# Layer 1 of a two-layer cross-attention kernel: keys, tokens and cluster tiles turned on VectorE and through DRAM instead of on TensorE

## The chip, the cores and the metric

One core of a Trainium2 chip. The metric is device microseconds (us) of one execution of the whole program, float32 throughout. The kernel before ran three times: 1796.07, 1797.0 and 1801.03 us, median 1797.0. Engines in the views: PE is TensorE's matrix multiplication, PEld its weight loads, DVE is VectorE, ACT ScalarE, POOL GpSimd, SP SyncE, which here does nothing but issue DMAs.

## The reference

`x` is 32 batches of 64 tokens of 512 elements, `ctx` the same shape. Two layers run one after the other, each with an attention to `ctx` and a feed-forward part. Layer 0 (one wide attention head, a sparse feed-forward part) is not touched by the change. Layer 1 is:

```
def xattn(h, ctx):                     # h = layernorm(x)
    q = (h @ Wq.T)  -> 32 heads of 128
    k = (ctx @ Wk.T), v = (ctx @ Wv.T) -> 8 groups of 128
    q = rmsnorm(q) * q_norm_w          # over the 128 of a head
    k = rmsnorm(k) * k_norm_w          # each group serves 4 heads
    p = softmax(q @ k.T / sqrt(128) + mask)
    return (p @ v) @ Wo.T
def ffn(h):                            # h = layernorm(x), 2048 rows
    dots = softmax(h @ centroids.T / 0.1)         # 64 clusters
    hits = dots > 0.01
    row_sel = any(hits over rows)[assignments]    # per output column
    query_sel = any(hits over clusters)           # per row
    return where(query_sel & row_sel, h @ weight.T + bias, 0)
x = x + xattn(layernorm(x), ctx)
x = x + ffn(layernorm(x))
```

## The kernel before

**Residency.** `x` stays in SBUF as 16 tiles `X[t]` of 128 rows (two batches) by 512. A matrix product contracts over the 128 partitions, so whatever enters a product must first stand "turned", with the contracted dimension on partitions. Before, this turning is a TensorE transpose: a matmul against the identity matrix from SBUF into PSUM, followed by a copy back to SBUF on ScalarE or VectorE. `transposed` (L181 its matmul) does four of them for a 128x512 tile.

**Units.** Layer 1 is cut into 32 units: T = 0 to 3 (512 tokens each, eight batches) by g = 0 to 7 (a key and value group with its four query heads). The four large projections are done by Winograd's scheme: seven products of 2x2 blocks in place of eight, with sums of inputs formed on GpSimd (`four_sums`, L127), each product two halves of four matmuls of 128x256 into a PSUM bank `b` (L901). One product takes TensorE 1.73 us, one projection 12.1 us.

- `project_kv` runs for every second unit and makes keys and values of two groups, in the layout tokens on partitions (`kv`).
- `project_q` runs for each unit and makes the turned queries `qT` from the turned, normalised tokens `xt` and their sums `tx`.
- `normed_keys`, `applied_norms` and `turned_keys` run once per pair of units: sums of squares of the keys, the reciprocal root (`ss`), a product `kn = kv * ss` (L1022), four transposes into PSUM `ptk` (L1033), and a scaling from PSUM by the column `wkc` (both norm weights and the 1/sqrt(128)) into `kT` (L1035), twice.
- `query_norms` gets the queries' sums of squares with small matmuls (L1048) and a VectorE transpose by 32x32 blocks (L1054).
- `softmax` has 32 small matmuls of 64x64 per half (L1070), `turn` turns the probabilities by 32x32 blocks on VectorE and DMAs between partitions (L1108 and L1116), `attend` multiplies by the values (L1130), `project_out` adds into `X` (L1161).

**Order.** The loop over units is a hand-written software pipeline: in iteration n stand the attention of unit n-1, the scores of unit n, `project_kv` (for an even g) and `project_q` of unit n+1, then `project_out` of unit n-1, in the middle of which the keys of the next pair were turned. `tc.issue_after` pins an instruction behind another on the same or another engine; what is not pinned is placed by a list scheduler. SP issues its DMAs in one order for the whole program, and a DMA that waits holds all behind it. Weights for T = 0 come from the inputs, with their sums made on GpSimd and stored to DRAM (`keep_sum`, L887); for T = 1 to 3 they are read (L880).

**Tokens.** `tokens(T)` normalises four tiles of `X` (`layernorm`: L104, L105, L114, L115 and L108 for `xn`), transposes them in the midst of `project_kv` (`amid`), copies them to `xt` on ScalarE (L924) and sums on GpSimd. For T = 0 this stands at the start of layer 1, with no other unit beside it.

**Clusters.** For tiles 0 to 11, `turn_and_keep` normalises the finished `X[t]`, transposes it (L181, `pt4`), copies it to `xT4` (L1182) and writes that to DRAM (`XTS`); `clusters` multiplies it with the centroids `CE` (L1198, `pl`) a unit later, two tiles at a time, in units 25 to 30. After the loop the twelve tiles are read back (L1316) for the dense product `pd` (L1350); tiles 12 to 15 are turned in the tail.

**Buffers.** The work tag `xn1` has two buffers of 128x512 and serves `xn` and, in the last unit, one half of `tb`. The PSUM tag `p1` has two banks, shared by `ptx`, `ptk1`, `pt4`, `pl` and half of the attention's results.

Of the kernel before, what the change touches and what calls it, by code (L numbers as in the profile page):

```python
# [16 lines left out]
P = 128  # L17
# [18 lines left out]
def tile_kernel(  # L36
# [801 lines left out]
    with ExitStack() as pc:  # L838
# [16 lines left out]
        ones32 = wk.tile([P, 32], F32, name="ones32", bufs=1)  # L855
        nc.vector.memset(ones32, 1.0)

        first_sums, context_sums, kv_products, softmaxes, projected = [], [], [], [], []
# [48 lines left out]
        def sbuf_keep(n, ps):  # L907
            e = wk.tile([P, 2, 256], F32, name=f"keep{n}", tag="keep", bufs=4)
            keeps.append(nc.scalar.copy(e, ps).ins)  # L909
            return e  # L910

        def tokens(T):


            xt = cpool.tile([P, C, 512], F32, name=f"xt_{T}", tag="xt")

            def normed(k):
                for a in (2 * k, 2 * k + 1):
                    xn = wk.tile([P, D], F32, name="xn1", tag="xn1")
                    layernorm(xn, 4 * T + a)  # L920
                    pt = ps_1.tile([P, C, P], F32, name="ptx", tag="p1")
                    with tc.issue_after(kv_products[2 if T == 0 else -1]):
                        transposed(pt, xn)
                    nc.scalar.copy(xt[:, :, a * P : (a + 1) * P], pt)  # L924

            def summed():
                q = [xt[:, 2 * i : 2 * i + 2, 256 * j : 256 * j + 256] for i in range(2) for j in range(2)]
                s = [cpool.tile([P, 2, 256], F32, name=f"tx_{T}_{k}", tag=f"tx_{k}") for k in range(4)]

                with tc.issue_after(context_sums[0]) if T == 0 else ExitStack():  # L930
                    first_sums.append(four_sums(nc.gpsimd, s, *q, True))
                return q + s

            return normed, summed

# [8 lines left out]

        def project_kv(cts, gp, T, amid=None):

# [4 lines left out]
            def mm(i, ps, first):  # L951
                if amid is not None and i in (7, 3):
                    amid((7, 3).index(i))
                last = products(ps, lambda h, c: cts[LEFT[i]][:, h, c, :], lambda h, c: w[i][:, c, :], first)
                kv_products.append(last.ins)
                projected.append(last.ins)
                if T == 0:
                    keep_sum(w, i, WKS, gp, True, last)
# [53 lines left out]

        def applied_norms(kvs, ss, behind, rooted):

            with tc.issue_after(rooted) if rooted is not None else ExitStack():
                nc.scalar.activation(ss, ss, AF.Sqrt, bias=eps5, scale=1.0 / HD)
            with tc.issue_after(behind[0]), tc.issue_after(behind[-1]):
                nc.vector.reciprocal(ss, ss)
            kns = []
            for k, kv in enumerate(kvs):  # L1020
                kn = wk.tile([P, 4, HD], F32, name="kn", tag="ksq", bufs=2)
                nc.vector.tensor_mul(kn, kv[:, :, 0:HD], ss[:, k, :, None].to_broadcast([P, 4, HD]))  # L1022
                kns.append(kn)
            return kns

        def turned_keys(kns, behind):

            kTs = []
            for kn in kns:
                pt = ps_1.tile([P, 4, P], F32, name="ptk1", tag="p1")  # L1030
                for a in range(4):
                    with tc.issue_after(behind):
                        nc.tensor.transpose(pt[:, a, :], kn[:, a, :], ident)  # L1033
                kT = wk.tile([P, 512], F32, name="kT1", tag="kT1")
                nc.vector.tensor_scalar(kT, pt.rearrange("p a t -> p (a t)"), wkc, None, ALU.mult)  # L1035
                kTs.append(kT)
            return kTs
# [22 lines left out]
        def softmax(h, qT, kT, ss, behind):  # L1060
# [3 lines left out]
            for a in range(2):  # L1064
                for j in range(J):
                    for b in range(2):
                        bb = 2 * (2 * h + a) + b
                        at = 2 * (2 * h + b) + a
                        with tc.issue_after(behind):
                            score = nc.tensor.matmul(  # L1070
                                sc[b * S : (b + 1) * S, 4 * a + j, :], qT[:, at, j, :],
                                kT[:, bb * S : (bb + 1) * S], start=True, stop=True,
                            )
# [99 lines left out]
        hit = wk.tile([P, NT], F32, name="hit", bufs=1)  # L1173
        XTS = [dram.tile([P, C, P], F32, name=f"xts_{t}", tag=f"xts_{t}") for t in range(12)]

        def turned(t, out, behind=None):
            xn = wk.tile([P, D], F32, name="xn1", tag="xn1")
            applied.append(layernorm(xn, t))
            pt = ps_1.tile([P, C, P], F32, name="pt4", tag="p1")
            with tc.issue_after(behind) if behind is not None else ExitStack():  # L1180
                transposed(pt, xn)
            nc.scalar.copy(out, pt)  # L1182

        def turn_and_keep(t):
            out = wk.tile([P, C, P], F32, name="xT4", tag="xT4", bufs=2)
            turned(t, out)
            nc.sync.dma_start(XTS[t], out)
            return out

        def clusters(t, tiles, behind=None):  # L1190

            pl = ps_1.tile([P, 2, NCL], F32, name="pl", tag="p1")
            for m in range(2):
                for c in range(C):
                    for k in range(2):
                        half = slice(k * P // 2, (k + 1) * P // 2)
                        with tc.issue_after(behind) if behind is not None else ExitStack():
                            nc.tensor.matmul(  # L1198
                                pl[half, m, :], tiles[m][:, c, half], CE[:, c, :], start=c == 0,
                                stop=c == C - 1, skip_group_check=True,  # L1200
# [32 lines left out]
        with tc.high_priority(offset=100):  # L1233
            normed, sums_of = tokens(0)
            normed(0)
            normed(1)
            xts = sums_of()
        kns = normed_keys(kvs)
        qT, qsq = project_q(xts, 0, 0)
        kTs = turned_keys(applied_norms(kvs, kns, puts[:1], None), projected[-3])  # L1240
        kT = kTs[0]
# [10 lines left out]
        for n, (T, g) in enumerate(units):  # L1252
# [14 lines left out]
            if more:  # L1267
# [3 lines left out]
                if g2 == 0:  # L1271
                    normed, sums_of = tokens(T2)
                    kvs = project_kv(cts, 0, T2, normed)
                    xts = sums_of()
# [19 lines left out]
            if more and g2 % 2 == 0:  # L1294
                with tc.high_priority(offset=60):
                    kTs = turned_keys(
                        applied_norms(kvs, kns, puts[-2:], keeps[-2]), outs[-5] if before is not None else projected[-1]
                    )
            kT = kTs[g2 % 2]
# [4 lines left out]
            t = 2 * (n - 24)  # L1304
            pair = (t, [turn_and_keep(t), turn_and_keep(t + 1)]) if 0 <= t < 12 else None
            if n == 23:
# [6 lines left out]
        nc.sync.dma_start(WD, wd)  # L1313
        xT = [fpool.tile([P, C, P], F32, name=f"xT4_{t}") for t in range(NT)]
        for t in range(12):
            nc.sync.dma_start(xT[t], XTS[t])  # L1316
        bdb = wk.tile([P, D], F32, name="bdb", tag="rt", bufs=1)
# [24 lines left out]
        def dense(t, parts=1):  # L1342


            for h in range(parts):
                cols = slice(D // parts * h, D // parts * (h + 1))
                pd = ps_j.tile([P, D // parts], F32, name="pd", tag="pj")
                for c in range(C):
                    with tc.issue_after(dense_at[-1]) if dense_at else ExitStack():
                        ins = nc.tensor.matmul(  # L1350
                            pd, xT[t][:, c, :], WD[:, c, cols], start=c == 0, stop=c == C - 1
                        )
# [150 lines left out]
```

## Time and profile before

The profile is of one execution, which took 1799.84 us; its span, from the first to the last instruction, is 1798.1 us, with 1.74 us around it.

| what | value |
|---|---|
| time of the profiled execution / its span | 1799.84 us / 1798.1 us |
| median of the runs | 1797.0 us |
| layer 0, up to the first layer 1 matmul | 556.16 us from the span's start |
| one period of layer 1 (two units) | 71.58 us |
| PE busy | 1773.8 us, 11364 instructions |
| VectorE / ScalarE / GpSimd busy | 968.0 / 623.0 / 715.4 us |
| DMA | 219.31 MB, mean 122 GB/s |
| granted TensorE clock, mean | 0.999 of full speed |

How to read it: busy time of an engine is the sum of its instructions' listed durations, overlaps counted once. A matmul's end is modelled, so that what PE really spends on a row of matmuls is the distance between starts. A line of a timeline has the start, the duration, the engine, the source line, the operation, the tiles written and read, the shapes, and the count of instructions merged; a bracket gives idle time before it and what ended that. In the table by stretches each engine has its busy time and, in brackets, its instructions; the last three numbers are the granted clock, the share of the DMA engines' time and GB/s. The chain of waits follows the last instruction back to what released it, step by step.

### The profile page before, as it was taken

The numbers are of one execution on the slowest core, as the hardware profiler recorded it, in microseconds if no ns is written. First come the engines' busy times: TensorE is split into PE (matmuls) and PEld (weight loads), VectorE is DVE, ScalarE is ACT, GpSimd is POOL, SyncE is SP. The second block draws the span as 40 slices with busy tenths as digits, with TensorE's granted clock in tenths as the row PEclk, the third lists the DMA queues.
The fourth block names the chain that finished last, engine by engine and source line by source line (L and its number), as shares of the span: only waits on it lengthen the run. The fifth ranks groups of instructions, "written<-read, shape, count | busy, mean of one in ns | idle before, by whom it ended". The sixth has DMA issues, their size and how long they took to land.

```text
span 1798.1 us, 29543 instructions
## 1 busy us (share of the span) xinstructions
PE 1773.8 (99%) x11364; PEld 1446.9 (80%) x11364; DVE 968.0 (54%) x1733; ACT 623.0 (35%) x1157; POOL 715.4 (40%) x622
## 2 busy tenths in 40 slices
PE   8999999999999999999999999999999999999999
PEld 4544988988998788888888888888888888888864
DVE  5887565555524454455455444555554555555557
ACT  4654322222112423334234333442343433433311
POOL 1552433443327766764324234332243332322320
PEclk9999999999999999999999999999999999999999
DMA  9632400000014344454444454444445444443513
GB/s 248 195 108 66 166 23 22 22 22 21 13 55 148 130 158 152 141 194 153 147 147 130 143 162 126 132 147 136 135 131 163 137 129 143 149 146 117 182 48 94
DMA packets 169500, 219.31 MB, mean 122 GB/s; under 512 B 19024, under 2 KB 108112, under 8 KB 168720
## 3 DMA queue, kind: packets, MB, share of 16 engines
q1 hardware_dynamic: 155712, 206.91, 37.1%
q10 hardware_dynamic: 13648, 10.50, 2.0%
q8 instruction: 91, 1.49, 0.4%
q14 instruction: 49, 0.40, 0.1%
HBM read 176.74 MB, written 32.21 MB: 116 GB/s over the span
## 4 chain that ended last, share of the span: by engine, by line
PE 88%; POOL 4%; DMA 3%; DVE 2%; ACT 1%; issue 1%; SPq 0%; POOLq 0%; ACTq 0%; DVEq 0%
PE b L901 49%; PE ph L727 10%; PE po L770 10%; PE pv L1130 3%; PE sc L1070 3%; PE pd L1350 3%; PE pq L397 3%; POOL so L127 2%; PE pk L374 2%; PE pr L1048 1%; PE pt L181 1%; PE pi L279 1%; POOL prob L1077 1%; DMA x<-in_x 1%; DMA wos<-wo 1%; PE ptk L1033 1%
## 5 line engine op out<-in xcount | busy, mean ns | idle before, releaser
L1161 DVE TENSOR_TENSOR x<-x,b 128x512 f32<-128x512 f32 x224 | 153.9, 687 | 228.7 <-PE b L901 228.7
L127 POOL TENSOR_TENSOR so<-oT 128x512 f32<-128x512 f32 x64 | 80.1, 1273 | 485.0 <-ACT oT L1137 485.0
L901 PE MATMUL b<-tx,wq 128*128 128x256 f32 x1024 | 237.8, 380 | 3.2 <-DVE qT L994 1.7
L901 PE MATMUL b<-wo,so 128*128 128x256 f32 x1024 | 231.7, 379 | 1.8 <-issue 1.8
L901 PEld LDWEIGHTS b<-tx,wq 128*128 128x128 f32 x1024 | 193.9, 190 | 31.9 <-POOL tx L127 2.5
L901 PEld LDWEIGHTS b<-wo,so 128*128 128x128 f32 x1024 | 194.5, 190 | 28.6 <-issue 2.2
L901 PE MATMUL b<-xt,wq 128*128 128x256 f32 x768 | 183.5, 381 | 0.9 <-DVE kv L965 0.9
L901 PE MATMUL b<-wo,oT 128*128 128x256 f32 x768 | 181.5, 379 | 0.0
L901 PEld LDWEIGHTS b<-xt,wq 128*128 128x128 f32 x768 | 144.4, 190 | 21.2 <-DVE kv L965 1.3
L901 PEld LDWEIGHTS b<-wo,oT 128*128 128x128 f32 x768 | 144.8, 190 | 19.9 <-issue 1.0
L909 ACT COPY keep<-b 128x512 f32<-128x512 f32 x144 | 83.8, 583 | 181.7 <-PE b L901 178.8
L1137 ACT COPY oT<-pv 128x512 f32<-128x512 f32 x64 | 37.4, 584 | 280.6 <-PE pv L1130 270.8
L994 DVE TENSOR_TENSOR qT<-b,keep 128x512 f32<-128x512 f32 x96 | 66.1, 689 | 116.9 <-PE b L901 114.5
L901 PE MATMUL b<-wkv,sc 128*128 128x256 f32 x512 | 117.0, 380 | 0.0
L1082 DVE TENSOR_REDUCE mx<-prob 128x8 f32<-128x512 f32 x64 | 43.9, 686 | 125.0 <-POOL prob L1077 125.0
L901 PEld LDWEIGHTS b<-wkv,sc 128*128 128x128 f32 x512 | 96.6, 190 | 13.8 <-issue 1.0
L272 POOL TENSOR_TENSOR e<-e,down 128x896 f32<-128x896 f32 (+1 forms) x40 | 68.0, 1706 | 93.9 <-DVE e L268 89.8
L997 ACT ACTIVATE qsq<-qT 128x512 f32<-128x512 f32 x128 | 80.3, 627 | 70.5 <-DVE qT L994 58.6
L770 PE MATMUL po<-w,gT 128*128 128x256 f32 x448 | 101.9, 382 | 0.0
L1094 POOL TENSOR_TENSOR prob<-prob,mx 128x512 f32<-128x512 f32 x64 | 66.5, 1060 | 86.0 <-DVE mx L1093 83.6
L770 PEld LDWEIGHTS po<-w,gT 128*128 128x128 f32 x448 | 84.0, 190 | 18.7 <-issue 7.8
L901 PE MATMUL b<-wkv,ct 128*128 128x256 f32 x384 | 93.0, 384 | 2.6 <-DVE mx L1093 2.0
(211 smaller groups left out, 3053.0 us busy)
## 6 DMA issues: line engine op xcount, KB each, us to landing
wq<-in_wq SPq DMA_DIRECT2D x104, 256.0 KB
wo<-in_wo SPq DMA_DIRECT2D x104, 256.0 KB
wq<-wqs SPq DMA_DIRECT2D x96, 256.0 KB
wo<-wos SPq DMA_DIRECT2D x96, 256.0 KB
wkv<-in_wkv SPq DMA_DIRECT2D x52, 256.0 KB
wkv<-wks SPq DMA_DIRECT2D x48, 256.0 KB
wqs<-wq SPq DMA_DIRECT2D x32, 256.0 KB
aT<-tb ACTq DMA_DIRECT2D x256, 32.0 KB
```

The costliest lines, as they stand in the source:

```text
L127: ins = eng.tensor_tensor(s[k], *pairs[k], op)
L272: nc.gpsimd.tensor_tensor(e3, e3, down[:, None, :].to_broadcast([P, k, BLK]), ALU.mult)
L397: nc.tensor.matmul(pq, xT[:, tt, c, :], WQ[:, c, :], start=c == 0, stop=c == C - 1)
L727: nc.tensor.matmul(ps[:, c, :], W1[LEFT[i]][:, d, (c0 + c) * P : (c0 + c + 1) * P], xq[RIGHT[i]][:, d, :], start=first and c == 0 and d == ...
L770: nc.tensor.matmul(ps, chunk(gq[LEFT[i]], c), W2[RIGHT[i]][:, c, :], start=first and c == 0, stop=c == HC - 1, skip_group_check=True,)
L901: last = nc.tensor.matmul(out[:, h, :], lhs(h, c), rhs(h, c), start=first and h == 0 and c == 0, stop=c == 1, skip_group_check=True,)
L909: keeps.append(nc.scalar.copy(e, ps).ins)
L994: ins = nc.vector.tensor_add(o, ps, kept.rearrange("p j (b t) -> p j b t", t=S))
L997: nc.scalar.activation(qsq[:, 4 * th : 4 * th + 4, 2 * hh : 2 * hh + 2, :], o, AF.Square)
L1070: score = nc.tensor.matmul(sc[b * S : (b + 1) * S, 4 * a + j, :], qT[:, at, j, :], kT[:, bb * S : (bb + 1) * S], start=True, stop=True,)
L1094: ins = nc.gpsimd.tensor_tensor(pr, pr, mx[:, 1, :, None].to_broadcast([P, 8, S]), ALU.mult)
L1161: added.append(nc.vector.tensor_add(xq[:, i, j], xq[:, i, j], ps).ins)
```

## The change

Everything that layer 1 turned on TensorE before tile 12 of the clusters is turned in another way: VectorE transposes a 128x512 tile by 32x32 blocks, with the blocks put in an order that makes rows of 128 elements (`to_dram`), SP writes the 256 KB to DRAM, and four DMAs read it back into 32 partitions each (`from_dram`), in pieces of 512 bytes. The two steps together are the whole transpose.

- Keys: `applied_norms` and `turned_keys` become one function. The norm weights are no longer a column after the transpose; they are a row `wkrow`, the same on all partitions, multiplied in with the norm by a `scalar_tensor_tensor` per head of 128. `wkrow` is made once, by four small matmuls `pw` of `ones32` with the diagonal matrix `wkd`, and four copies. `kT` now lies as `[p, q, a, x]`, in runs of 32.
- Tokens: `norm_tokens` normalises and writes `XND[T]`; for T = 1 to 3 it is called in units g = 4 and 5 of the T before. `tokens` reads it. `xt` lies as `[p, 16, c, 32]`; the sums use views of it, and `tx` has the layout as before.
- Clusters: tiles 0 to 11 go through `XTS`, which now is one tensor, and are read back for `clusters` at once and again after the loop. Their layout is `[p, row, c]`, so that the stationary operand of `pl` and `pd` takes every fourth element. `xT` becomes one tile, `xTs`, of all 16; tiles 12 to 15 still use TensorE, and their copies write the new layout.

In the changed kernel's order of TensorE, the four `pw` stand after the last matmul of layer 0 and before the first product of `project_kv`.

```diff
+        wkd = wk.tile([P, P], F32, name="wkd", tag="xn1")
+        nc.vector.tensor_scalar(wkd, ident, wkc, None, ALU.mult)
+        wkrow = wk.tile([P, HD], F32, name="wkrow", bufs=1)
+        for r in range(4):
+            pw = ps_1.tile([32, P], F32, name="pw", tag="p1")
+            nc.tensor.matmul(pw, ones32, wkd, start=True, stop=True)
+            nc.scalar.copy(wkrow[32 * r : 32 * r + 32, :], pw)
...
+        def to_dram(rows, src, order, name):
+            tb = wk.tile([P, D], F32, name=name, tag="xn1")
+            to = {"c h": "p (h c x) -> p c h x", "x c": "p (h x c) -> p c h x"}
+            nc.vector.transpose(
+                tb.rearrange(to[order], h=4, x=32), src.rearrange("p (c h x) -> p c h x", h=4, x=32)
+            )
+            return nc.sync.dma_start(rows, tb)
+        def from_dram(dst, rows):
+            for h in range(4):
+                nc.sync.dma_start(
+                    dst[32 * h : 32 * h + 32],
+                    rows[:, P * h : P * h + P].rearrange("(q l) x -> l q x", l=32),
+                )
+        def norm_tokens(T, a):
+            xn = wk.tile([P, D], F32, name="xn1", tag="xn1")
+            layernorm(xn, 4 * T + a)
+            to_dram(XND[T][a * P : (a + 1) * P, :], xn, "c h", "tbx")
...
         def tokens(T):
-                    with tc.issue_after(kv_products[2 if T == 0 else -1]):
-                        transposed(pt, xn)
-                    nc.scalar.copy(xt[:, :, a * P : (a + 1) * P], pt)
+            xt = cpool.tile([P, 16, C, 32], F32, name=f"xt_{T}", tag="xt")
+            from_dram(xt.rearrange("p q c x -> p q (c x)"), XND[T])
...
-                nc.vector.tensor_mul(kn, kv[:, :, 0:HD], ss[:, k, :, None].to_broadcast([P, 4, HD]))
...
-                        nc.tensor.transpose(pt[:, a, :], kn[:, a, :], ident)
-                kT = wk.tile([P, 512], F32, name="kT1", tag="kT1")
-                nc.vector.tensor_scalar(kT, pt.rearrange("p a t -> p (a t)"), wkc, None, ALU.mult)
+                for a in range(4):
+                    nc.vector.scalar_tensor_tensor(
+                        kn[:, a, :], kv[:, a, 0:HD], ss[:, k, a : a + 1], wkrow, ALU.mult, ALU.mult
+                    )
+                to_dram(KTD[k], kn.rearrange("p a d -> p (a d)"), "c h", "tbk")
+                kT = wk.tile([P, 4, 4, 32], F32, name="kT1", tag="kT1")
+                from_dram(kT.rearrange("p q a x -> p q (a x)"), KTD[k])
...
         def turn_and_keep(t):
-            out = wk.tile([P, C, P], F32, name="xT4", tag="xT4", bufs=2)
-            turned(t, out)
-            nc.sync.dma_start(XTS[t], out)
+            for m in range(2):
+                xn = wk.tile([P, D], F32, name="xn1", tag="xn1")
+                layernorm(xn, t + m)
+                to_dram(XTS[(t + m) * P : (t + m + 1) * P, :], xn, "x c", "tbc")
+            out = wk.tile([P, 2, P, C], F32, name="xT4", tag="xT4", bufs=1)
+            from_dram(out.rearrange("p m (q x) c -> p (m q) (x c)", x=32), XTS[t * P : (t + 2) * P, :])
...
-                                pl[half, m, :], tiles[m][:, c, half], CE[:, c, :], start=c == 0,
+                                pl[half, m, :], tiles[m][:, half, c], CE[:, c, :], start=c == 0,
...
+            if T < 3 and g in (4, 5):
+                for a in (2 * g - 8, 2 * g - 7):
+                    norm_tokens(T + 1, a)
...
-        xT = [fpool.tile([P, C, P], F32, name=f"xT4_{t}") for t in range(NT)]
-        for t in range(12):
-            nc.sync.dma_start(xT[t], XTS[t])
+        xTs = fpool.tile([P, NT, P, C], F32, name="xTs")
+        for t, n in ((0, 2), (2, 4), (6, 6)):
+            from_dram(
+                xTs[:, t : t + n].rearrange("p m (q x) c -> p (m q) (x c)", x=32), XTS[t * P : (t + n) * P, :]
+            )
...
-                            pd, xT[t][:, c, :], WD[:, c, cols], start=c == 0, stop=c == C - 1
+                            pd, xT[t][:, :, c], WD[:, c, cols], start=c == 0, stop=c == C - 1
```

## The prediction

> **What bounds the kernel now.** I read the page's first part, then the chain, then a table by stretches, then timelines where the edits land. The first two, from the page:
>
> ```profile
> PE 1773.8 (99%) x11364; PEld 1446.9 (80%) x11364; DVE 968.0 (54%) x1733; ACT 623.0 (35%) x1157; POOL 715.4 (40%) x622
> ...
> PE 88%; POOL 4%; DMA 3%; DVE 2%; ACT 1%; issue 1%; SPq 0%; POOLq 0%; ACTq 0%; DVEq 0%
> ```
>
> The table by stretches, here for one period of layer 1 (two units of work):
>
> ```profile
> core 0: us, PE busy (x) PEld busy (x) DVE busy (x) ACT busy (x) POOL busy (x), PEclk, DMA share, GB/s
> ...
> 1003.17:1074.75 71.58, 71.58 (x465) 61.00 (x464) 35.27 (x58) 25.85 (x41) 27.97 (x24) 1.00 0.51 151
> ```
>
> PE holds 88% of the chain, and in the period it is busy throughout at a granted clock of 1.00, while VectorE is busy for 35.27 of 71.58 us and the DMA engines for half. So in the steady part PE time taken away is time saved, and VectorE has 36 us free per period. Only the edges of layer 1 are not of this kind.
>
> **What is removed.** PE loses 240 transposes: 128 of keys, 64 of tokens, 48 for the cluster tiles 0 to 11. Their listed 273 ns is no price, since modelled ends overlap. The price is the step between starts, on PE's timeline (start, duration, count last):
>
> ```profile
> 1002.31 1.03 PE L901 MATMUL b<-wo,so 128*128 128x256 f32 x4
> 1003.17 1.04 PE L1033 MATMUL ptk<-ident,kn 128*128 128x128 f32 x8
> 1004.04 1.89 PE L901 MATMUL b<-wo,oT 128*128 128x256 f32 x8
> ```
>
> Eight transposes hold PE from 1003.17 to 1004.04: 0.87 us, or 109 ns each. Keys: 16 such groups, 13.9 us. Tokens: 64 x 0.109 = 7.0. Cluster tiles: 48 x 0.109 = 5.2. Together **-26.1 us**. With T=1's token copies ACT is also freed; on PE's timeline 0.90 us is lost at 844.13, waiting for ACT's `keep` in that stretch: **-1**.
>
> VectorE loses 32 `kT` scalings (L1035, 22.5 us) and 32 products `kn` (L1022, 22.9). It gains 60 block transposes, at the 704 ns of L1108's `tb`, 42 us, and 128 products of 128x128. No row shows that product; L744's 384-element form takes 609 ns and its 512-element form 746, so a line through them gives about 0.26 us, 33 us in all. Net +30 us on an engine busy for 968 of 1798.
>
> **Keys, in the steady part: hidden.** They now go VectorE, DRAM, SBUF. In the period shown the reciprocal of the keys' norms runs at 997.07. Eight products and two transposes (8 x 0.26 + 2 x 0.70), interleaved with x's additions, end at about 999.2 and 1001.3. A 256 KB write takes about 2 us from issue to the last packet (the `wo` load issued at 1003.37 ends at 1005.6), so the copies lie in DRAM at 1001 and 1003.2. Eight reads follow on SP, 0.33 to 0.38 us each to issue, and about 1 us for 512 packets: `kT` is there at about 1005 and 1006. The first score starts at 1013.97, 0.87 earlier once the transposes are gone. Slack: **7 us**. Behind these DMAs on SP stands the weight load issued at 1001.64, now about 1005.3; its product is a whole unit later. Cost 0.
>
> Tokens of T=1 to 3 are written one to two units ahead and read about 17 us before their use: 0. Cluster tiles of one pair keep only 2 to 3 us of slack, the others a unit: 0, with a bound of +3.
>
> **T=0: the part that shows.** Here no unit runs beside the chain. Before, PE's order is:
>
> ```profile
> 553.14 3.18 PE L770 MATMUL po<-w,gT 128*128 128x256 f32 x14
> 556.16 1.89 PE L901 MATMUL b<-wkv,ct 128*128 128x256 f32 x8
> ...
> 568.40 1.89 PE L901 MATMUL b<-wkv,ct 128*128 128x256 f32 x8
> 570.13 1.89 PE L901 MATMUL b<-xt,wq 128*128 128x256 f32 x8
> ```
>
> and what VectorE and GpSimd do in it:
>
> ```profile
> 555.29 2.49 POOL L127 TENSOR_TENSOR sc<-ct 128x512 f32<-128x512 f32 x2 [5.20 <-DMA ct<-in_cT]
> ...
> 556.36 0.42 DVE L778 TENSOR_TENSOR x<-x,po 128x256 f32<-128x256 f32 x1 [1.69 <-PE po L770]
> 556.70 1.10 DVE L853 TENSOR_TENSOR wkc<-colt 128x1 f32<-128x1 f32 x1
> ...
> 557.75 1.27 POOL L127 TENSOR_TENSOR sc<-sc,ct 128x512 f32<-128x512 f32 x1
> ```
>
> First, the four matmuls `pw` of the key weights' row stand in PE's order ahead of `project_kv`. They wait for `wkd`, which follows `wkc` on VectorE; the 128x1 product took 1.10 us, to the end of GpSimd's two sums at 557.78, and `wkd` likewise waits for the third, which ends at 559.0. Then four matmuls go with copies between them (two PSUM buffers, L461's 266 ns): keys' projection starts at 559.6 to 560.5 instead of 556.16, **3.4 to 4.3 us late**.
>
> Second, the token chain. Without 16 transposes `project_kv` would end at 568.4, and 4 us later at 572.4; then `project_q` needs `xt`. Each of four tiles takes a normalisation, a transpose and a write of about 2 us, and the transposes share two buffers with what they read, so each waits for the write before it: about 2.2 to 2.7 us a tile from 560.5. The last write is issued at about 568 to 570.5 and landed 2 us later. Then the reads: 2048 packets of 512 B. The nearest row is `ch<-choice` (64 KB issues at 171.26 to 178.7, 512-B packets): 1792 packets in 8.0 us, 224 per us, and 400 per us at its densest. So 5.1 to 9.1 us, and `xt` is there at 575.5 to 581; I take 577.5, from the early write and a rate near 350, since four large issues leave no gaps as the sixteen small ones do. Against 568.4 the whole boundary costs **+9.1** (7 to 13).
>
> Third, the clock. The table by stretches after an earlier place with gaps (third number from the right: granted clock):
>
> ```profile
> 178.90:182.40 3.50, 3.50 (x16) 1.89 (x15) 3.20 (x6) 0.00 (x0) 2.17 (x2) 0.51 0.86 262
> 182.40:190.00 7.60, 7.60 (x70) 7.60 (x70) 2.10 (x5) 2.32 (x5) 0.00 (x0) 1.00 1.05 396
> ```
>
> After gaps of about 1 us between 174 and 180 the granted clock was 0.51 for 3.5 us, a loss of 1.7. Two idle stretches of 4 to 5 us may each do this: 0 to 3.4, I take **+1.7**. The weight loads and GpSimd's sums of T=0 run in another order against `project_q`; **+1** (-2 to +4).
>
> **Stationary operands at a 16-byte stride.** Cluster tiles now lie as `[p, row, c]`, so 256 weight loads of `pl` and 136 of `pd` pick every fourth element. No row of before has this. Below: 0, as nothing in it shortens a load. Above: `pl` runs at a 29 ns step (32 in 1.0 us from 1479.76), and were its loads four times as long as that step, 256 x 87 = 22 us. `pd` has a 429 ns step over loads listed at 190, so up to twice nothing shows. Nearest in kind are L1130 and L1048, whose moving operand comes in runs of 32 at no cost (390 against L901's 380), but runs are not single elements. I take a tenth of the upper end, **+2.5**, range 0 to 22.
>
> [...]
>
> **Tail.** `xTs` is one tile; its twelve reads become 6144 packets of 512 B, 15 to 27 us by the rates above from about 1688, and the `wo` loads stand behind them on SP (before issued from 1697.75). They are wanted at 1711.54, where 1.82 us is already lost: **+1** (0 to 6).
>
> **Sum.** -26.1 - 1 + 9.1 + 1.7 + 1 + 2.5 + 1 = -11.8. The profiled execution took 1799.84 us (span 1798.1 and 1.74 around it): 1788.0. It lies 2.8 above the median of the runs, 1797.0, so in medians **1785**. All favourable ends together give -22, 1775; all unfavourable ones, with the cluster tiles' +3 but the stride at 0, give +2, 1799.
>
> **Rivals.**
> 1. The T=0 chain is hidden (GpSimd's sums or other loads bind there anyway, `pw` is early): -11.8 - 10 = -22, **1775**. For: VectorE has free time. Against: `pw` is first in PE's order.
> 2. The boundary and the tail take their upper ends (+13, +3.4, +4, +6) and `pl`'s step grows by half (+4): -26.1 - 1 + 30.4 = +3, or **1800**: no change. For: writes and reads in series with two buffers. Against: it wants all of them late.
> 3. Slower: the keys' round trip. Each write, read and wait on SP's one queue is longer than I take it, because SP waits at the first write for VectorE and at the reads for the write's landing, with weight loads around them. It decides when `kT` lands over 7 us later than my 1006, a round trip of 14 us from the last transpose's 1001.3 to 1013.1 in place of 5. Each us later than that is paid in each of the 15 pairs after the first: 2 us late is 1785 + 30 = **1815**. For: every hop is serial and unshown. Against: the wait for DMA engines is small at a share of 0.51.
> 4. PE's work is not really less (the order puts other work in the transposes' place): **1797**. The instruction list speaks against it; a few in a hundred.
>
> **Chances.** Forecast (1777 to 1792) 0.60, first rival 0.11, second 0.14, third 0.12, fourth 0.03. A measurement here tells about 0.3% (5.4 us) from no change. Faster by more: 0.74 (forecast, first rival, a little of the second); within: 0.14; slower: 0.12. For 8 in 10 the range takes in the forecast, the first rival with 3 us below it, and the second: 1772 to 1801.
>
> **What would show it.** No PE gap in the steady period, about 70.7 us long instead of 71.58; `kT` landing 5 us or more ahead of the scores; gaps of about 4 us at 556 and 5 us before the first `project_q`, perhaps with a granted clock of 0.5; `pl`'s step of 29 ns, or twice that; the first `project_out` of the tail at about the same distance from the end. A PE wait ahead of the scores in every second unit would make the prediction wrong, as would a `pl` step over 60 ns.

## The result and the profile after

The changed kernel takes 1849.51 us (median of four runs, 1847.04 to 1850.62) against 1797.24 for the kernel before on the same chip: a ratio of 1.0285, 95% interval 1.0266 to 1.0304, **slower by 2.9%**. 1785 was forecast, with a range of 1772 to 1801. The profiled execution took 1850.27 us, its span is 1848.5.

First part and chain of the page of the changed kernel:

```profile
PE 1775.2 (96%) x11132; PEld 1455.6 (79%) x11132; DVE 1009.2 (55%) x1858; ACT 614.7 (33%) x1133; POOL 713.5 (39%) x622
...
PE 85%; POOL 5%; DVE 4%; DMA 3%; issue 1%; ACT 1%; SPq 0%; ACTq 0%; POOLq 0%; DVEq 0%
```

PE has 232 instructions less (240 transposes gone, eight records of `pw` added) and is busy as long as before: in place of the transposes stand a longer step of `pl` (experiment 4) and work at half clock, some 33 us of its busy time in layer 1. Its share falls from 99% to 96%. The table by stretches, first the period that answers to the one shown before, then three stretches in which the clock was halved:

```profile
core 0: us, PE busy (x) PEld busy (x) DVE busy (x) ACT busy (x) POOL busy (x), PEclk, DMA share, GB/s
1054.19:1124.90 70.71, 70.71 (x460) 60.17 (x457) 40.17 (x75) 26.46 (x43) 27.99 (x25) 1.00 0.54 173
575.69:585.93 10.24, 5.63 (x13) 4.56 (x14) 3.39 (x9) 0.59 (x1) 5.97 (x6) 0.50 0.78 179
678.09:684.92 6.83, 6.15 (x15) 4.91 (x16) 2.78 (x7) 3.10 (x5) 5.79 (x6) 0.50 0.04 10
1746.46:1763.53 17.07, 5.07 (x12) 4.08 (x13) 2.11 (x3) 1.24 (x2) 1.06 (x2) 0.50 0.72 184
```

In the steady part the change does what was forecast: 70.71 us in place of 71.58, PE busy throughout. The loss is elsewhere. PE's waits in the units of T=0 and the first of T=1 (window 600 to 930) of the changed kernel, in total, times and the longest:

```profile
PE b L908 <- DVE qT L1018: 17.1, 4, 4.9
PE b L908 <- DVE kv L989: 5.3, 3, 3.9
PE b L908 <- DVE x L1178: 4.5, 2, 2.7
PE b L908 <- DVE mx L1110: 2.0, 2, 1.1
```

Before, the wait for `qT` in the same window was

```profile
PE b L901 <- DVE qT L994: 1.7, 1, 1.7
```

And in the tail of the changed kernel (window from 1730):

```profile
PE b L908 <- DMA wo<-in_wo: 14.7, 1, 14.7
```

The best measure of where time goes is the start of a unit's scores on PE (`sc`), which both kernels have 32 times: the distance of the two starts, taken at a few units, cuts the loss into stretches. For the profiled executions, in us against before:

| stretch | after | what is in it |
|---|---|---|
| to the first scores | +13.5 | boundary of T=0 |
| first to tenth scores | +28.5 | the units of T=0, first of T=1 |
| tenth to 25th | -10.9 | steady part |
| 25th to 32nd | +0.9 | clusters |
| from the 32nd to the end | +18.5 | tail |
| sum | +50.4 | 1848.5 against 1798.1 |

The first row scatters by a few us between executions, since layer 0, which the change does not touch, ends anywhere from 552.8 to 557.6 us. The second row scatters too: experiments 1, 4 and 7 leave the code of these units as it is, and in their profiles it is 34.5, 30.0 and 27.5. The row from the tenth scores to the 25th is -11.0, -11.1 and -9.1 there. Each row is from one execution of a kernel; totals are compared by medians.

### The profile page after: what moved, and what is told of

The parts are those of the page before. It is cut to its first block, busy times and chain, and to the rows that moved or that the text cites. A ratio compares the mean times of both kernels' runs of the same rounds, so it can differ in the third digit from the quotient of the medians.

```text
span 1848.5 us, 29500 instructions
## 1 busy us (share of the span) xinstructions
PE 1775.2 (96%) x11132; PEld 1455.6 (79%) x11132; DVE 1009.2 (55%) x1858; ACT 614.7 (33%) x1133; POOL 713.5 (39%) x622
## 4 chain that ended last, share of the span: by engine, by line
PE 85%; POOL 5%; DVE 4%; DMA 3%; issue 1%; ACT 1%; SPq 0%; ACTq 0%; POOLq 0%; DVEq 0%
PE b L908 47%; PE ph L727 10%; PE po L770 9%; PE pq L397 3%; PE pv L1147 3%; PE pd L1373 3%; PE sc L1087 3%; PE pk L374 2%; POOL so L127 2%; PE pr L1066 1%; POOL wo L127 1%; POOL prob L1094 1%; PE pi L279 1%; DMA wo<-in_wo 1%; PE pl L1218 1%
## 5 line engine op out<-in xcount | busy, mean ns | idle before, releaser
L908 PE MATMUL b<-tx,wq 128*128 128x256 f32 x1024 | 243.3, 386 | 18.6 <-DVE qT L1018 17.1
L908 PEld LDWEIGHTS b<-tx,wq 128*128 128x128 f32 x1024 | 197.6, 194 | 48.7 <-DVE qT L1018 18.7
L908 PE MATMUL b<-wo,oT 128*128 128x256 f32 x768 | 185.5, 385 | 14.7 <-DMA wo<-in_wo 14.7
L908 PE MATMUL b<-xt,wq 128*128 128x256 f32 x768 | 187.3, 386 | 10.6 <-DMA xt<-xnd 9.5
L908 PEld LDWEIGHTS b<-wo,oT 128*128 128x128 f32 x768 | 149.0, 194 | 37.4 <-DMA wo<-in_wo 15.4
```

Source lines behind the costliest of these rows:

```text
L908: last = nc.tensor.matmul(out[:, h, :], lhs(h, c), rhs(h, c), start=first and h == 0 and c == 0, stop=c == 1, skip_group_check=True,)
```

## The experiments

**Theory**: SP's one queue. In the units of T=0 the keys' writes and reads stand ahead of the next output weights, which GpSimd must sum at once; the sums come late, the softmax stands behind them on GpSimd, PSUM is freed late, and a PE wait of some us is followed by a half-clock stretch (6.83 us at the wait of 4.4 near 674 in the changed kernel). In the tail the cluster reads stand ahead of the output weights. **Rivals**: VectorE's added products, held by GpSimd's instructions; the rate of the 512-byte reads; the order that the scheduler wrote for GpSimd.

In the expectations, `e3_tokens0_pe` is experiment 3 and `e6_sp_order` is experiment 6.

**1. The tail: weights ahead of the cluster reads.**

```diff
...
+        w_out = load_weights(o_quarter, WOS, before[1], before[0], True, "wo", 7)
         inputs.close()
...
-            project_out(ots, before[1], before[0])
+            project_out(ots, before[1], before[0], w_out)
```

> The changed kernel with one thing moved: in the tail, the weight loads of the last but one project_out are issued on SP ahead of the twelve reads of the cluster tiles. Theory (SP's one queue: the last two reads wait for a transfer of ScalarE's, and the weights stand behind them): PE's wait of 14.7 us before that project_out falls below 3, the half-clock stretch after it goes, and the time falls by 13 to 18 us, to 1832 to 1837. Rival (the 512-byte reads themselves are too slow): PE then waits for the tiles before the first dense product instead, and less than 5 us is gained.

Measured: 1840.26 us, ratio to before 1.0229 (1.0210 to 1.0248); 9.3 us less than the changed kernel by medians, and 11 by the distances of both to the runs of before on their own chips; 13 to 18 were expected. In the tail stretch the loss falls from 18.5 to 3.1 us, and PE's waits from 1690 on are now

```profile
PE b L908 <- issue: 1.1, 1, 1.1
PE pd L1375 <- DMA xTs<-xts: 0.5, 1, 0.5
```

The tiles are there in time, with a wait of 0.5 us, so the rate of the reads is not the cause; the queue is. The total fell by less than the tail did: in the profiled execution the units of T=0, which the edit does not touch, lost 34.5 us in place of 28.5: PE's waits there sum to 34.0 us in place of 28.9, and the half-clock stretches to 30.7 in place of 27.3. SP's waits of the changed kernel between 1700 and 1760 name what held the queue:

```profile
SPq L931 <- DMA aT<-tb: 26.9, 7, 20.3
SPq L931 <- PE b L908: 13.2, 1, 13.2
```

and its timeline shows where it stood:

```profile
1719.63 31.52 SPq L931 DMA_DIRECT2D xTs<-xts  x12
1751.52 0.35 SPq L1341 DMA_DIRECT2D bdb<-in_bd  x1
1754.77 0.40 SPq L887 DMA_DIRECT2D wo<-in_wo  x1
```

Ten of the twelve reads were out by 1729.4; the eleventh stood until 1750.2. It waited for the first of the last unit's later transfers of probabilities (`aT`), which ScalarE issued only at 1748.36, and the weights stood behind it. Before, the reads also waited for such a transfer, 15.1 us, but for one of a unit earlier. Why a read of the cluster tiles waits for such a transfer, no run shows; it was not varied.

**2. Keys of T=0 on PE.**

```diff
+                if on_pe is not None:
+                    pt = ps_1.tile([P, 4, P], F32, name="ptk1", tag="p1")
+                    for a in range(4):
+                        with tc.issue_after(on_pe):
+                            nc.tensor.transpose(pt[:, a, :], kn[:, a, :], ident)
+                    nc.vector.tensor_copy(kT..., pt...)
...
```

> The changed kernel with the keys of T=0 (and of the first pair of T=1, turned beside T=0's last unit) transposed on PE again, scaled by the row on VectorE as in the changed kernel; the other pairs go through DRAM. Theory (the keys' writes and reads hold SP's queue, so the next unit's output weights come late, GpSimd sums them late, and the softmax behind them in GpSimd's order is late): the PE waits of 3.7 to 5.0 us near 674, 758, 836, 870 and 918 us go, with their half-clock stretches; from the first scores to the tenth the loss of 28 us falls to under 3; the time falls by 25 to 30 us, to 1820 to 1825. Rival (VectorE's added products wait for GpSimd and make the softmax late): these products are still there, the waits stay, and less than 8 us is gained.

Measured: 1834.06 us, 1.0193 (1.0177 to 1.0210), 15.5 us less than the changed kernel by medians where 25 to 30 were expected. The waits for `qT` near 674, 758, 836 and 918 are gone, and the stretch loses 11.8 us in place of 28.5: 17 us belong to the keys' way through DRAM. The wait near 870, which was also to go, is still there (3.8 us, for `kv`), and 11.8 us remain where under 3 were expected, in part in waits that the theory did not have. VectorE, PE and GpSimd of this kernel at one of them:

```profile
644.68 6.41 DVE L1048 SCALAR_TENSOR_TENSOR kn<-kv,ssk,wkrow 128x128 f32<-128x128 f32 x8
645.18 5.24 POOL L127 TENSOR_TENSOR wq<-wq,wq 128x512 f32<-128x512 f32 x4 [7.18 <-DMA aT<-tb]
645.37 1.89 PE L908 MATMUL b<-wo,oT 128*128 128x256 f32 x8
647.10 1.89 PE L908 MATMUL b<-wo,so 128*128 128x256 f32 x8
651.01 1.27 DVE L1188 TENSOR_TENSOR x<-x,b 128x512 f32<-128x512 f32 x2
651.83 2.41 PE L908 MATMUL b<-wo,so 128*128 128x256 f32 x8 [2.85 <-DVE x L1188]
```

Eight products, with a median of 0.35 us each over the run, take 6.41 us beside four of GpSimd's sums; `x`'s addition stands behind them in VectorE's queue, and PE waits 2.85 us for the PSUM bank that it frees. So the rival looks right too, for the smaller part; experiments 5 and 8 try it.

**3. Tokens of T=0 on PE.**

```diff
...
+            if T == 0:
+                    ...
+                    with tc.issue_after(kv_products[2]):
+                        transposed(pt, xn)
+                    nc.scalar.copy(xt[:, 4 * a : 4 * a + 4]..., pt...)
+            else:
+                from_dram(xt.rearrange("p q c x -> p q (c x)"), XND[T])
```

> The changed kernel with the tokens of T=0 transposed on PE again; all else as changed. Theory (write after write through two buffers, then the reads, in series with nothing beside them): the wait of 9.5 us before the first project_q and the half clock after it go; the first scores come 10 to 13 us earlier, and the time falls by as much, to 1837 to 1840. Rival (the weights of T=0, late on the same queue, end that wait anyway): under 4 us is gained.

Measured: 1850.51 us, 1.0285 (1.0268 to 1.0303): no gain in the total. In the profile the wait of 9.5 us is gone and the loss to the first scores falls from 13.5 to 5.4 us, 1.2 of which is layer 0, which ended earlier; but the next stretch loses 32.4 in place of 28.5, which is within its scatter. The saving at the boundary does not show in the total; experiment 9 returns to it.

**4. Cluster tiles read as if contiguous.**

```diff
-                                pl[half, m, :], tiles[m][:, half, c], CE[:, c, :], start=c == 0,
+                                pl[half, m, :], tiles[m].rearrange("p t c -> p (t c)")[:, P * c + k * P // 2 : P * c + (k + 1) * P // 2], CE[:, c, :], start=c == 0,
...
-                            pd, xT[t][:, :, c], WD[:, c, cols], start=c == 0, stop=c == C - 1
+                            pd, xT[t].rearrange("p t c -> p (t c)")[:, P * c : P * c + P], WD[:, c, cols], start=c == 0, stop=c == C - 1
```

> The changed kernel, in which pl and pd read the same cluster tiles as if they lay contiguously by c, in place of every fourth element (the numbers are then not those of the reference). Theory (a stationary operand at a 16-byte stride doubles a weight load): the step of pl goes from 59 ns back to 29, 320 of them are 256 x 0.030 = 7.5 us, and the time falls by 6 to 8 us, to 1841.5 to 1843.5; pd's step of 429 ns stays. Rival (the step is that of the tiles' late arrival or of the clock): the step stays at 59 ns and the time within 2 us.

Measured: 1845.41 us, 1.0259 (1.0238 to 1.0280). The weight loads of `pl` (minimum, median, maximum in ns), of the changed kernel and then of this one:

```profile
L1218 PEld LDWEIGHTS pl<-CE,xT x192: 193/217/218, 1509.9 to 1713.4; 128*64 128x64 f32 x192
```

```profile
L1218 PEld LDWEIGHTS pl<-CE,xT x192: 132/138/138, 1514.7 to 1711.3; 128*64 128x64 f32 x192
```

By starts, 32 loads and products take 1.80 to 1.86 us at the stride and 0.88 without it: 59 and 29 ns. Six groups of 32 and one of 64 (256 in all; the 320 of the expectation is a slip) cost 7.5 us by that, the cluster stretch fell by 6.9 and the tail by 2.5. `pd` keeps its 429 ns. The total fell by 4.1 us by medians and 6.3 by the distances to the runs of before, at the lower edge of what was expected or below it; the step is shown by the loads, not by the total.

**5. Four scaling products in place of eight.**

```diff
+                nc.vector.tensor_mul(kn, kv[:, :, 0:HD], ss[:, k, :, None].to_broadcast([P, 4, HD]))
+                nc.vector.tensor_mul(kn, kn, wkrow[:, None, :].to_broadcast([P, 4, HD]))
```

> The changed kernel with the keys' scaling in two products of 128x512 a tile (norm, then row) in place of four of 128x128: four VectorE instructions a pair in place of eight. Theory (beside GpSimd's weight sums at T=0 every SBUF-to-SBUF product on VectorE waits for the end of a GpSimd instruction, 6.4 us for eight in the run with T=0's keys on PE): four wait about half as long, the PE waits of 1.9 to 2.9 us in project_out near 648 and 729 us shrink below 1 us, and the time falls by 3 to 7 us, to 1843 to 1847. Rival (it is VectorE's own work): the work is the same 2.8 us, and the time stays within 2 us.

Measured: 1856.80 us, 1.0311 (1.0293 to 1.0330), 7 us more than the changed kernel by medians, with intervals that touch; neither theory nor rival had that. The stretch of T=0 loses 29.7 us, about what it lost in the changed kernel (28.5), and the two waits in project_out are still 1.8 us each. Halving the count of instructions did not help: the first two take 1.29 us, all but 0.2 of it ahead of GpSimd's sums, the last two 3.44 us beside them. The profiled execution, the slowest of the four, is 11 us longer than that of the changed kernel: 5.4 at the boundary (2.7 of it layer 0), 1.1 in T=0, 1.4 in the steady part (0.35 us in four of its eight pairs) and 3.3 with the clusters. This was not followed.

**6. Only SP's order changed.** The reads of the keys get an edge behind the next unit's last load of output weights.

```diff
...
+                if tag == "wo":
+                    for d in key_dmas:
+                        tc.add_manual_dep(d.ins, load.ins.name, NOSYNC, reason="keys behind the weights")
...
```

> The changed kernel with only SP's order changed: the eight reads of a pair's keys stand behind the next unit's loads of output weights instead of ahead of them. Theory (SP's queue makes the weights of T=0 late): the first GpSimd sum of those weights starts 4 us or more earlier against the scores, the PE waits of 3.7 to 5.0 us near 674, 758, 836 and 918 us fall below 2, and the time falls by 10 to 17 us, to 1833 to 1840; the steady part stays as it is. Rival (GpSimd's fixed order, with weight sums between the parts of a softmax, decides whatever the loads do): the waits stay above 3 us and less than 5 us is gained.

Measured: 1832.88 us, 1.0190 (1.0170 to 1.0210), by medians 16.6 us less than the changed kernel, as the theory had it. PE's waits between 600 and 930:

```profile
PE b L912 <- DVE x L1184: 5.8, 3, 2.8
PE b L912 <- DVE kv L995: 5.2, 3, 3.7
PE b L912 <- DVE qT L1024: 3.8, 4, 1.2
...
PE sc L1093 <- DMA kT<-ktd: 1.1, 1, 1.1
```

Four waits for `qT` take 3.8 us in place of 17.1, and the stretch loses 11.6 us in place of 28.5. What this order costs is also there: once, the scores wait 1.1 us for the keys. On GpSimd, of the changed kernel first, the same unit:

```profile
662.44 1.28 POOL L127 TENSOR_TENSOR wo<-wo,wo 128x512 f32<-128x512 f32 x1 [11.98 <-DMA wo<-in_wo]
...
671.03 1.26 POOL L1094 TENSOR_TENSOR prob<-prob,msk 128x512 f32<-128x512 f32 x1
672.26 1.26 POOL L127 TENSOR_TENSOR wo<-wo,wo 128x512 f32<-128x512 f32 x1
673.49 1.25 POOL L1094 TENSOR_TENSOR prob<-prob,msk 128x512 f32<-128x512 f32 x1
```

```profile
664.28 2.62 POOL L127 TENSOR_TENSOR wo<-wo,wo 128x512 f32<-128x512 f32 x2 [10.07 <-PE b L912]
...
675.96 2.51 POOL L1100 TENSOR_TENSOR prob<-prob,msk 128x512 f32<-128x512 f32 x2
```

Against the unit's scores (661.73 and 668.78) the first sum starts 0.7 us after them and 4.5 us before them; before the change it was 4.5 before as well. The changed kernel has a weight sum between the two halves of the softmax, this one has not: the scheduler's order for GpSimd changed with SP's. So late loads and GpSimd's order are not told apart, but both follow from SP's order.

**7. Clusters undone.** `turned`, `turn_and_keep`, the reads after the loop and both products as in the kernel before.

```diff
-            for m in range(2):
-                ...
-                to_dram(XTS[(t + m) * P : (t + m + 1) * P, :], xn, "x c", "tbc")
...
+            out = wk.tile([P, C, P], F32, name="xT4", tag="xT4", bufs=2)
+            turned(t, out)
+            nc.sync.dma_start(XTS[t], out)
```

> The changed kernel with the clusters' part undone: tiles 0 to 11 are transposed on PE, laid contiguously and read back as before; keys and tokens as changed. Theory (this part costs more than its 5.2 us of transposes bring: 7.5 us by pl's step, 15 to 18 us in the tail behind SP's reads): the PE wait of 14.7 us in the tail goes, pl's step is 29 ns, and the time falls by 18 to 23 us, to 1826 to 1832. Rival (the tail waits for something else): less than 10 us is gained.

Measured: 1832.47 us, 1.0176 (1.0160 to 1.0193), 17 us less by medians and 18.6 by the distances to the runs of before. `pl`'s loads take 138 ns, and the tail loses 0.0 us in place of 18.5. The clusters' way through DRAM, meant to take away 5.2 us, costs some 18 net.

**8. On top of SP's order: two scaling products a pair.**

```diff
-                    nc.vector.scalar_tensor_tensor(
-                        kn[:, a, :], kv[:, a, 0:HD], ss[:, k, a : a + 1], wkrow, ALU.mult, ALU.mult
-                    )
+                nc.vector.tensor_mul(kn, kv[:, :, 0:HD], ss[:, k, :, None].to_broadcast([P, 4, HD]))
```

> The kernel of e6_sp_order (key reads behind the weight loads on SP) with the keys scaled as before the change, by one product of 128x512 a tile with the norm alone: two VectorE instructions a pair, and the row of the key weights is left out of the computation. Theory (at T=0 the rest of the loss is the longer scaling on VectorE running into GpSimd's weight sums, which begin about 2 us after it starts; x's additions stand behind it): the two products are done before the sums begin, as in the kernel before; the PE waits of 2.9 us at 652 and 730 us fall below 0.5, their half-clock stretches of 3.4 us go, and against e6_sp_order the time falls by 7 to 10 us, to 1823 to 1826; the wait of 3.9 us at 863 us stays (GpSimd's token sums ahead of the softmax). Rival (the block transposes or the writes on SP hold x's additions): the waits stay above 2 us and less than 4 us is gained.

Measured: 1827.53 us, 1.0168 (1.0150 to 1.0186), 5.4 us less than experiment 6 by medians, where 7 to 10 were expected; the two intervals overlap. The first to tenth scores lose 2.7 us in place of 11.6, and PE's waits for `x` are 0.3 us in place of 5.8:

```profile
PE b L912 <- DVE kv L995: 5.7, 3, 4.2
PE b L912 <- DVE qT L1024: 4.1, 4, 1.2
...
PE b L912 <- DVE x L1181: 0.3, 1, 0.3
```

The place of this kernel that answers to the one shown in experiment 2:

```profile
644.23 2.37 DVE L1053 TENSOR_TENSOR kn<-kv,ssk 128x512 f32<-128x512 f32 x2
644.75 5.55 POOL L127 TENSOR_TENSOR wq<-wq,wq 128x512 f32<-128x512 f32 x4 [7.21 <-DMA wqs<-wq]
647.74 0.65 DVE L1181 TENSOR_TENSOR x<-x,b 128x512 f32<-128x512 f32 x1
```

The products are not over before the sums begin, as the theory had it: they run 1.9 us into them. They hold VectorE for 2.37 us in place of 6.41, and that is enough for `x`'s addition to be in time. How much of the difference is the meeting with GpSimd and how much the six products fewer was not separated. The longest wait for `kv` (4.2 us, at 851) stays, as expected. The total fell by less than the stretch did, and the two profiles are the slowest of experiment 6's four executions and the fastest of this kernel's, so the 8.9 us of the stretch may be too much.

**9. On top of SP's order: tokens of T=0 on PE.** The edits of experiments 6 and 3 together.

> The kernel of e6_sp_order with the tokens of T=0 transposed on PE, as in e3_tokens0_pe. Theory (what e3_tokens0_pe saved at the start of layer 1 was given back by longer half-clock stretches at the later waits of T=0, which are mostly gone here): the first scores come 9 to 12 us earlier than in e6_sp_order, and most of it stays to the end: 1821 to 1826. Rival (the token path through DRAM only moves the wait to other loads of T=0): under 4 us against e6_sp_order.

Measured: 1829.22 us, 1.0167 (1.0149 to 1.0186), 3.7 us less than experiment 6, where 7 to 12 were expected: the rival's "under 4". The first scores come 8.9 us earlier, but 2.8 of that is layer 0, which ended earlier in this execution; of the 8.9, 4.4 is left at the tenth. In place of the one wait for tokens PE has six of 0.6 to 1.8 us between 560 and 625, for weights, their sums on GpSimd, `qsq`, the probabilities' transfers, the first keys (1.1 us), and once for nothing that the profile shows: the wait for tokens had covered what else was late. So the rival holds for the larger part of the boundary's saving. What else was lost in experiment 3 stays open, within the scatter of the half-clock stretches, which come in pieces of 3.4 us.

**10. The change kept only where it brings something.** Keys through DRAM from the second pair of T=1 on, tokens for T=2 and 3, clusters as before; `wkrow` is made after T=0.

```diff
+                        (outs[-5] if before is not None else projected[-1]) if T == 0 else None,
...
+                    kvs = project_kv(cts, 0, T2, normed if T2 <= 1 else None)
...
-            if T < 3 and g in (4, 5):
+            if 1 <= T < 3 and g in (4, 5):
```

> The change kept only where it was seen to bring something: keys through DRAM from the second pair of T=1 on (11 of 16 pairs), tokens through DRAM for T=2 and 3; T=0, T=1's tokens and the clusters as in the kernel before; the row of the key weights is made at the end of T=0. Theory (the loss lies at T=0, in the first unit of T=1 and in the clusters alone): the distance to the kernel before is 0 up to the tenth scores, then falls by 0.87 us a pair and by 2.1 us a token set; 11 x 0.87 + 2 x 2.1 = 13.8, that is 1783 to 1786. Rival (the DRAM path also costs in the steady part, hidden by the other waits): within 5 us of the kernel before.

Measured: 1788.59 us against 1798.84, ratio **0.9935 (0.9919 to 0.9952)**: faster than both kernels, and above the 1783 to 1786 that were expected. The distance to before is at most 0.06 us from the second scores to the eighth, and from the tenth it falls by 0.88 a pair and by 2.98 where a pair and a token set come together, to -9.6 us; 13.8 was expected. Most of the difference is one place: at the tenth scores it stands at +3.2. Both kernels have a PE wait near 881 (2.0 and 1.7 us, for `qT`); here a half-clock stretch of 3.4 us follows it, with PE at work throughout (1.7 us lost), before none does. Another 1.7 us or so go to the four `pw` for `wkrow`, which now stand among the products of the attention just ahead of the tenth scores; the expectation had no term for them.

## Why the prediction was wrong, point by point

**Right.** The price of a transpose, 109 ns: the steady part falls by 0.87 to 0.88 us a pair. The keys' round trip is hidden there; the third rival, the only one that would have made the kernel slower, is not what happened. Tokens of T=2 and 3 are hidden (2.98 less 0.88 is 2.1 us each). In the stretch from the tenth to the 25th scores 11.2 us were to be had (8 x 0.875 + 2 x 2.1) and 10.9 came.

**Wrong, the main step: the rest of T=0 at "+1 (-2 to +4)".** It cost 28.5 us: between the first and the tenth scores PE's waits sum to 28.9 us, 6.4 before, and 22.7 us of its work at half clock cost 11 more, less the transposes gone. The prediction followed the delayed weight load in the steady part, where "its product is a whole unit later. Cost 0", and for T=0 gave the other order of loads and sums no more than this +1. At T=0 a load's first reader is not the product but GpSimd's sum, and that stands in GpSimd's order ahead of the softmax of the unit. 17 us of it are SP's order (experiments 2 and 6). Another 5 (by the medians of the totals) to 9 (11.6 to 2.7 in the stretch) are VectorE's scaling, by experiment 8: the prediction counted VectorE's added work, the eight products among it, as +30 us on an engine with room, when what counts is whether `x`'s additions behind them are in time. Before, at the same place, the two products of `kn` were over when the sums began:

```profile
631.97 1.29 DVE L1022 TENSOR_TENSOR kn<-kv,ssk 128x512 f32<-128x512 f32 x2
633.76 5.19 POOL L127 TENSOR_TENSOR wq<-wq,wq 128x512 f32<-128x512 f32 x4 [8.47 <-DMA aT<-tb]
```

The +30 itself was misworked: a line through 609 ns at 384 elements and 746 at 512 gives 0.335 us at 128, not 0.26. The products' median is 0.346, and VectorE's busy time grew by 41 us.

What holds the long products of experiment 2 was not separated; the runs show what goes with them. In the changed kernel the products' median is 346 ns, the longest 1420, with GpSimd's sums at 1.27 us each: at 728.45 three products take 3.40 us beside three of these sums, at 577.54, with GpSimd idle, three take 0.83. The prediction read such a wait off a row for `wkd` and did not ask about the eight products.

**Tokens of T=1 at 0.** Their sums no longer wait for the transposes inside `project_kv`, and on GpSimd they now stand ahead of a softmax, in the changed kernel

```profile
861.15 1.27 POOL L127 TENSOR_TENSOR tx<-xt,tx 128x512 f32<-128x512 f32 x1
...
863.61 1.26 POOL L127 TENSOR_TENSOR tx<-xt,tx 128x512 f32<-128x512 f32 x1
864.84 1.26 POOL L1094 TENSOR_TENSOR prob<-prob,msk 128x512 f32<-128x512 f32 x1
```

where before they stood behind it:

```profile
837.53 2.42 POOL L1094 TENSOR_TENSOR prob<-prob,mx 128x512 f32<-128x512 f32 x2 [2.84 <-DVE mx L1093]
839.91 2.50 POOL L127 TENSOR_TENSOR tx<-xt 128x512 f32<-128x512 f32 x2
```

PE then waits 3.7 to 5.3 us for `kv`, from a start between 851 and 878, in every run with these tokens through DRAM. The wait is gone in experiment 10, where they are on PE; no run changed them alone.

**The boundary at +9.1 (7 to 13), the clock at +1.7.** The first row of the table, 13.5, holds both, after a layer 0 that happened to end 2.3 us early, less 1.7 for the transposes gone: some 17.5 us where 10.8 were summed. The last write was issued at 568.5 as forecast, but landed after 4.2 us, not 2, with stores and loads of weights beside it on the same queue; the reads took 5.8 us for 2048 packets, about 350 per us, as forecast. Layer 1's first product comes 3.3 us late (1.8 of it a wait for `wkd`), PE waits 9.5 us for `xt`, where 5 were forecast, and loses half of 5.63 busy us to the clock. Size off, mechanism right. What was not foreseen is the clock at the later waits: five stretches of 3.4 to 6.8 us between the boundary and the tail, and 17.1 in it.

**The stride at +2.5.** It was 7.5 by steps. A tenth of the upper end was a choice without a row behind it, and the rows of other operands were no guide. The step of `pl` doubled, from 29 to 59 ns (experiment 4).

**The tail at +1 (0 to 6).** It was 18.5, of which 2.5 are `pl`'s step by experiment 4. The prediction priced the reads' packets, which the runs show to be in time, and not the wait in the middle of them for a transfer of another engine, though the trace of before has that wait, 15.1 us long.

## What to carry to other kernels

In these runs, moving work from the bound engine to a queue was free where the queue's next entries had slack (a gain of 0.87 to 0.88 us a pair in the steady part) and not where they had none (some 17 us lost at T=0 by experiments 2 and 6): ask for each transfer that is pushed back who reads it first, and do it anew for the stage with another reader (here GpSimd's sums at T=0). A queue that keeps its order delayed, by a wait in it, what stood behind (in the changed kernel's tail SP's reads waited 20.3 us, and PE 14.7 for the weights behind them), so put loads that have long been ready to go ahead of a round trip, not behind. Where a change pays in the steady part and costs at the edges, apply it to the steady part alone.

## What was not expected of the hardware

A PE wait of a few us cost clearly more than its length where a stretch at half clock came with it, as with five of the six waits of 2.7 to 4.9 us in the units of T=0 and the first of T=1 of the changed kernel. The granted clock was 0.50 in pieces of 3.41 us: 3.41 or 6.83 at these waits, 10.24 and 17.07 at those of 9.5 and 14.7. At the wait of 4.4 us near 674 PE worked for 6.15 of the 6.83 us, so some 3 us came on top. It did not come with each: the wait of 3.5 us near 837 has no such stretch, while one of 2.0 in experiment 10 has 3.41 us. And a weight load of `pl` whose elements lie 16 bytes apart had twice the step, 59 ns in place of 29, while `pd`'s loads at that stride, listed at 308 ns in place of 190, showed nothing under its step of 429 ns.
